# A block's transposes moved into the next block's x projection, and a group's scores moved behind the gate

## The chip, the cores and the metric

The kernel runs on one core of one Trainium2 chip. The metric is the device time of one execution in microseconds, as the median of several runs. All times below are of one core.

## The reference, cut to what matters

The program is one layer of a hybrid model on 4 sequences of 256 tokens with 512 channels (1024 tokens in all): causal attention with 32 heads and an adapter, a small gated feed-forward layer, a state-space mixer with 128 heads of 64 channels in 8 groups, and the feed-forward layer again. The change lies in the mixer. There the reference computes:

```python
proj = input_states @ in_proj_w.T            # gate | x, B, C | dt
xBC  = silu(conv(xBC) + conv_b)              # causal, 4 taps, each channel for itself
...
scores  = einsum('bcihn,bcjhn->bcijh', C, B) * Ldec * dt
y_intra = einsum('bcijh,bcjhp->bcihp', scores, xc)
...                                          # plus the state carried between chunks, plus D * x
g = y * silu(gate)
g = g * rsqrt(mean(g * g over the group) + eps) * norm_w
return g @ out_w.T
```

B and C belong to a group of 16 heads; Ldec is the exponential of differences of cumulated decays. The kernel computes the state-space part over a whole sequence as one masked product: scores of C and B, times exponentials of decay differences, times x scaled by dt.

## The kernel before, in words

**Blocks and groups.** The mixer's 8192 channels are 64 blocks of 128 channels, two heads each (`NB`); 8 blocks make a group (`GB`). For block `i`, `g` is its group and `gi` its place in the group, 0 to 7. The activations lie channel by token, 128 x 1024 to a tile. float32 products are made of three matmuls on split operands (`mm3`, lines 115 to 117), so that a projection of 128 channels is 2 halves (512 tokens each) of 12 matmuls of 128x512.

**What a block does**, in the order in which `block(i)` writes it:

- the x projection (`projected("x", i, ...)`), two halves into a PSUM tile `pp` of two; between the halves it calls what it was given;
- `conv`: ScalarE's first tap (L964), VectorE's three taps (L971), ScalarE's Silu (L975) give `x2`;
- in blocks with `gi` 2 to 6, and in all of group 0, the output products `outer` of the group before (24 matmuls into `pog`, slots of tag "m", added to x by L1115), and around them `inner_products(i - 1)`: 32 matmuls of 128x64 weights (L1044, tile `pyy`) and then `gated` (L1054 to L1067);
- the gate projection (`projected("g", i, between)`). In the blocks with `gi` 7, 0 and 1 of later groups (`late`) `between` runs `inner_products(i - 1)` and `outer` between the gate's halves;
- the Silu of the gate (L1211), and `differences` of the two heads: VectorE (L1004), a mask on GpSimd (L1008) and exponentials on ScalarE (L1013, L1014, L1016) in `em`;
- `turned(i, x2)`: 8 transposes of x2 on TensorE (L1027, tile `trx`, two slots of tag "m"), and two VectorE multiplies by dt into `xd` (L1030);
- in blocks with `gi` 3 and 4 the B or C projection and convolution of the next group (`convolved`);
- `weighted`: `em` times the group's scores `gm` (L1020).

**Scores.** A group's `scores` are four pairs of matmuls (L986, L990, tile `pg`, slots of tag "m"), each followed by a VectorE multiply into `gm` (L991). They belong to the first block of a group (`gi` 0): two pairs between the x halves, two between the gate halves, ahead of the products of the block before.

**Order.** In group 0 a scheduler orders all engines. From block 8 on TensorE's instructions stand in the order written (`manual_schedule`), while the scheduler orders VectorE, ScalarE, GpSimd and SP's loads by its own forecast of the times. Every engine works through its own order and waits where an input or a slot is missing. The "m" slots are two, for `trx`, `pg`, `pog` and the sums `pqs`; `xd` has one buffer, `em` four, `x2` two.

**Tables.** ScalarE's Silu, exponential and square root need different function tables; a change between them is an ACT_TABLE_LOAD.

Of the kernel before, what the change touches and what calls it, by code (L numbers as in the profile page):

```python
# [29 lines left out]
NB = INTER // P  # L30
# [49 lines left out]
def hybrid_kernel(  # L80
# [12 lines left out]
    x = keep.tile([P, TT, C], F32, name="x")  # L93
# [11 lines left out]
    def split(hl, v, engine=nc.vector):  # L105

        nc.scalar.copy(hl[0], v)  # L107
        engine.tensor_tensor(hl[1], v, hl[0].bitcast(F32), ALU.subtract)
# [20 lines left out]
    class Norm:  # L129
# [33 lines left out]
        def turn(self, xn, tr, xs):  # L163

            for k in range(KC):
                nc.tensor.transpose(tr[:, k, :], xn[:, k * P : (k + 1) * P], ident)
            split(xs, tr)
# [618 lines left out]
    def mixer(feed, later):  # L786
        with ExitStack() as es, ExitStack() as inner:
# [25 lines left out]
            def prepare(i):  # L813

                for n in range(i, i + 3):
                    fetch(n)
                if i < NW and i not in pieces:
                    pieces[i] = [pw.tile([P, KC, P], F32R, name=f"w{j}", tag=f"w{j}") for j in range(2)]
                    split(pieces[i], raws.pop(i), nc.gpsimd if i < 18 or order[i][1] % GB in (7, 0) else nc.vector)

            def project(w, pp, cols):
                mm3(pp[:, cols], [[v[:, k, :] for v in w] for k in range(KC)],
                    [[v[:, k, cols] for v in xs] for k in range(KC)])
# [137 lines left out]
            def conv(pp, ch, tag, bufs):  # L961

                acc = (po_ if tag == "gb" else p2).tile([P, NT], F32, name="acc", tag=tag, bufs=bufs)
                nc.scalar.activation(  # L964
                    acc, pp, AF.Identity, bias=cb_s[:, ch : ch + 1], scale=cw_s[:, ch, 3:4]
                )
                av = acc.rearrange("p (b t) -> p b t", b=B)
                pv = pp.rearrange("p (b t) -> p b t", b=B)
                for tap in range(3):
                    d = 3 - tap  # L970
                    nc.vector.scalar_tensor_tensor(  # L971
                        av[:, :, d:], pv[:, :, : L - d], cw_s[:, ch, tap : tap + 1], av[:, :, d:],
                        ALU.mult, ALU.add,
                    )
                silus.append(nc.scalar.activation(acc, acc, AF.Silu).ins)  # L975
                return acc
# [45 lines left out]
            def turned(n, x2):  # L1022

                xd = p2.tile([P, TT, P], F32, name="xd", tag="xd", bufs=1)
                trs = [ps.tile([P, 4, P], F32, name="trx", tag="m") for _ in range(2)]
                for c in range(TT):
                    nc.tensor.transpose(trs[c // 4][:, c % 4, :], x2[:, c * P : (c + 1) * P], ident)  # L1027
                for half, tr in enumerate(trs):
                    hs = slice(half * 4, half * 4 + 4)
                    nc.vector.tensor_tensor(  # L1030
                        xd[:, hs, :].rearrange("p c (h d) -> p c h d", h=2),
                        tr.rearrange("p c (h d) -> p c h d", h=2),
                        dt_t[:, hs, 2 * n : 2 * n + 2].unsqueeze(3).to_broadcast([P, 4, 2, PD]),
                        ALU.mult,
                    )
                return xd

            def product(xd, es2):
                py = ps_y.tile([P, B, L], F32, name="pyy", tag="pyy")
                for b in range(B):  # L1040
                    for k in range(2):
                        for hh in range(2):
                            d = slice(hh * PD, (hh + 1) * PD)
                            nc.tensor.matmul(  # L1044
                                py[d, b, k * P :], xd[:, 2 * b + k, d],
                                es2[hh][:, b, 2 * k : 2 if k == 0 else 3, :].rearrange("p s i -> p (s i)"),
                                start=(k == 0), stop=(k == 1),
                            )
                return py
# [77 lines left out]
            def projected(kind, n, between=lambda: None):  # L1127
                i = at[kind, n]
                prepare(i + 1)
                prepare(i + 2)  # L1130
                w = pieces.pop(i)
                if i == 0:
                    return first[1]
                pp = (
                    ps_y.tile([P, NT], F32, name="pp", tag="pyy") if (kind, n) == ("g", 0)
                    else ps_p.tile([P, NT], F32, name="pp", tag="pp")
                )
                for half in range(2):
                    project(w, pp, slice(half * 512, half * 512 + 512))
                    if half == 0:  # L1140
                        between()
                return pp
# [7 lines left out]
            def outer():  # L1150

                q, t, hl = recalled.pop(0)
                po = ps.tile([P, C], F32, name="pog", tag="m")
                for half in range(2):
                    partial(po, q, hl[half], half)
                if t == 0:
                    rgs[q] = root(sqs.pop(q))
                scaled(q, t, po)

            def inner_products(m):  # L1160
                px2, gt, xd, em = stage.pop(m)
                py = product(xd, em)
                sqs[m // GB] = gated(m, px2, gt, py, sqs.get(m // GB))
# [8 lines left out]
            stage, sqs, wos, rgs, todo = {}, {}, {}, {}, []  # L1172
            recalled = []
            PER = {1: 1, 2: 2, 3: 1, 4: 1, 5: 2, 6: 1}
            def block(i, scoring, gm):
                g, gi = divmod(i, GB)
                if gi == 0 and g:
                    scoring = scores(group["b"], group["c"])
                    gm = next(scoring)
                    todo.extend((g - 1, t) for t in range(TT))  # L1180

                def scored():

                    for _ in range(2 if gi == 0 and g else 0):
                        next(scoring)

                x2 = conv(projected("x", i, scored), i, "x2", 2)

                late = gi in (7, 0, 1) and g > 0
                if not late:
                    if recalled:
                        outer()
                    if i:
                        inner_products(i - 1)
                    while recalled:
                        outer()
                if gi == 6:
                    wos.setdefault(g, []).extend(out_weights(g, k) for k in range(3))  # L1200

                def between():
                    scored()
                    if late:
                        inner_products(i - 1)
                        while recalled:
                            outer()

                pp = projected("g", i, between)
                gt = p2.tile([P, NT], F32, name="gt", tag="gt", bufs=1)  # L1210
                nc.scalar.activation(gt, pp, AF.Silu)  # L1211
                em = []
                for h in (2 * i, 2 * i + 1):
                    with tc.issue_after(silus[2]) if i == 0 else ExitStack():
                        em.append(differences(h, rr.pop(h)))
                    if h + 2 < H:
                        rr[h + 2] = rows(h + 2)
                xd = turned(i, x2)
                if gi in NEXT and g + 1 < G:
                    convolved(NEXT[gi], g + 1)  # L1220
                for e in em:
                    weighted(e, gm)
                stage[i] = (x2, gt, xd, em)
                for _ in range(PER.get(gi + 1, 0)):
                    if todo:
                        q, t = todo.pop(0)
                        recalled.append((q, t, [recall(q, t, half) for half in range(2)]))
                if gi == 7:
                    wos[g].extend(out_weights(g, k) for k in range(3, 6))
                if gi == 0 and g:  # L1230
                    wos[g - 1].extend(out_weights(g - 1, k) for k in range(6, 8))
                return scoring, gm
# [3 lines left out]
            with tc.manual_schedule(engines={nc.tensor.engine}):  # L1236
                for i in range(GB, NB):
                    scoring, gm = block(i, scoring, gm)
            inner_products(NB - 1)
            wos[G - 1].extend(out_weights(G - 1, k) for k in range(6, 8))  # L1240
            es_p.close()
# [48 lines left out]

    later = ExitStack()
    mixer(attention(later), later)


# [67 lines left out]
```

## Time and profile before

| | |
|---|---|
| runs | 1895.62, 1890.53, 1892.50 us; median 1892.5 |
| profiled execution | 1893.48 us; span from the first to the last instruction 1891.7 us, mean granted TensorE clock 0.987 |
| attention and feed-forward, up to the mixer's first block | about 410 us |
| mixer, blocks 0 to 7 | about 410 to 540 us |
| mixer, blocks 8 to 63 | about 540 to 1805 us, 181 us for a group of 8 blocks in groups 2 to 5 |
| rest (last output products, feed-forward) | about 1805 to 1892 us |

The page gives the busy time of each engine over the whole span. As TensorE's order is fixed from block 8 on, a gap on TensorE has one cause: the next instruction in its order lacks an input or a slot. In a timeline the time of a step is best read from the start of one matmul to the start of the next, since the ends of matmuls are modelled.

### The profile page before, as it was taken

To read this page: it belongs to the slowest core of one execution; us is meant where nothing else is said; L and a number is where in the kernel's file an instruction comes from. 1 tells how busy PE (TensorE), PEld (TensorE's weight loads), DVE (VectorE), ACT (ScalarE), POOL (GpSimd) and SP (SyncE) were. 2 spreads that over 40 slices of the span, in tenths; PEclk is the share of its full clock that TensorE was granted. 3 is DMA by queue.
4 is the path that set the end of the run, shared out by engine and by line. 5 is a ranking of instruction groups with operands and counts; after the bars stand their busy time and mean duration, and the time that the engine had idled before them with its cause. 6 is when DMAs were issued, how large, how long until landed. Compare 5 with 4: busy or idle time off the path is not lost.

```text
span 1891.7 us, 29927 instructions
## 1 busy us (share of the span) xinstructions
PE 1806.6 (96%) x10706; PEld 1454.4 (77%) x10706; DVE 1503.3 (79%) x2272; ACT 1425.3 (75%) x2851; POOL 459.7 (24%) x425
## 2 busy tenths in 40 slices
PE   8999988899999999999999999999999999999997
PEld 6777767677778887787788778877887788788777
DVE  5576667689998878887998788869878987897767
ACT  6666675379999768877887787778777976897654
POOL 6332230014442122212211311121222211321200
PEclk9999989899999999999999999999999999999999
DMA  4000000034565445543554455445544543554341
GB/s 143 1 1 1 22 15 25 24 101 156 172 199 184 142 135 170 175 150 124 177 184 144 141 161 176 148 143 167 170 134 155 184 152 123 165 186 156 101 120 54
DMA packets 152773, 240.35 MB, mean 127 GB/s; under 512 B 12464, under 2 KB 77616, under 8 KB 152624
## 3 DMA queue, kind: packets, MB, share of 16 engines
q1 hardware_dynamic: 152624, 238.44, 39.3%
q8 instruction: 84, 1.38, 0.3%
q14 instruction: 65, 0.53, 0.1%
HBM read 202.75 MB, written 35.65 MB: 126 GB/s over the span
## 4 chain that ended last, share of the span: by engine, by line
PE 61%; ACT 14%; DVE 13%; DMA 4%; issue 4%; POOL 3%; SPq 0%; DVEq 0%; ACTq 0%; POOLq 0%
PE pp L115 8%; PE pp L116 8%; PE pp L117 8%; PE pyy L1044 6%; PE pog L115 6%; PE pog L116 6%; PE pog L117 6%; DVE acc L971 3%; DMA wor<-in_wout_dram 2%; ACT e L477 2%; PE trx L1027 2%; DVE em L1020 1%; POOL sq L1067 1%; ACT em L1016 1%; ACT em L1013 1%
## 5 line engine op out<-in xcount | busy, mean ns | idle before, releaser
L115 PE MATMUL pp<-mx,w 128*128 128x512 f32 (+1 forms) x1160 | 463.7, 400 | 4.8 <-DVE acc L971 3.0
L116 PE MATMUL pp<-mx,w 128*128 128x512 f32 (+1 forms) x1160 | 452.4, 390 | 0.0
L117 PE MATMUL pp<-mx,w 128*128 128x512 f32 (+1 forms) x1160 | 452.3, 390 | 0.0
L971 DVE SCALAR_TENSOR_TENSOR acc<-pp,cw_s,acc 128x1012 f32<-128x1012 f32 (+2 forms) x240 | 303.8, 1270 | 70.1 <-ACT acc L964 67.9
L1020 DVE TENSOR_TENSOR em<-em,gm 128x1536 f32<-128x1536 f32 x128 | 254.6, 1992 | 40.1 <-ACT em L1016 40.1
L1008 POOL TENSOR_SCALAR_AFFINE_SELECT r<-r 128x512 f32<-128x512 f32 x128 | 127.2, 995 | 629.3 <-DMA r<-cumd 488.8
L115 PEld LDWEIGHTS pp<-mx,w 128*128 128x128 f32 x1160 | 219.1, 189 | 54.7 <-issue 8.3
L117 PEld LDWEIGHTS pp<-mx,w 128*128 128x128 f32 x1160 | 218.7, 189 | 46.4 <-issue 0.6
L116 PEld LDWEIGHTS pp<-mx,w 128*128 128x128 f32 x1160 | 219.2, 189 | 41.3 <-issue 0.6
L1067 POOL TENSOR_TENSOR sq<-sq,acc 128x1024 f32<-128x1024 f32 x55 | 149.7, 2722 | 355.1 <-ACT acc L1066 355.1
L115 PE MATMUL pog<-wo,gh 128*128 128x512 f32 x512 | 202.6, 396 | 0.0
L116 PE MATMUL pog<-wo,gh 128*128 128x512 f32 x512 | 199.5, 390 | 0.0
L117 PE MATMUL pog<-wo,gh 128*128 128x512 f32 x512 | 199.5, 390 | 0.0
L1004 DVE TENSOR_SCALAR em<-r,col_t 128x128 f32<-128x128 f32 x512 | 168.1, 383 | 28.3 <-PE pyy L1044 22.2
L1044 PE MATMUL pyy<-em,xd 128*64 128x256 f32 (+1 forms) x2048 | 183.4, 330 | 0.8 <-DVE em L1020 0.8
L1044 PEld LDWEIGHTS pyy<-em,xd 128*64 128x64 f32 x2048 | 129.9, 137 | 59.6 <-issue 17.5
L1013 ACT ACTIVATE em<-r,col_t 128x128 f32<-128x128 f32 x512 | 169.6, 391 | 6.2 <-PE pyy L1044 5.2
L1016 ACT ACTIVATE em<-r,col_t 128x128 f32<-128x128 f32 x512 | 170.3, 390 | 1.6 <-POOL r L1008 1.3
L107 ACT CAST w<-wr 128x512 fp32r<-128x512 f32 x144 | 88.4, 614 | 83.2 <-PE pp L116 79.6
L477 ACT ACTIVATE e<-sc,nmx 128x256 f32<-128x256 f32 (+1 forms) x256 | 104.2, 442 | 21.0 <-DVE nmx L471 20.9
L107 ACT CAST gh<-gr 128x512 fp32r<-128x512 f32 (+1 forms) x128 | 76.5, 607 | 52.8 <-PE pog L116 42.4
L115 PEld LDWEIGHTS pog<-wo,gh 128*128 128x128 f32 x512 | 96.1, 188 | 22.9 <-issue 3.8
(290 smaller groups left out, 3291.1 us busy)
## 6 DMA issues: line engine op xcount, KB each, us to landing
wr<-in_win_dram SPq DMA_DIRECT2D x287, 256.0 KB, 2.7
r<-cumd SPq DMA_DIRECT2D x128, 512.0 KB, 4.1
spill<-gb SPq DMA_DIRECT2D x63, 512.0 KB, 2.9
gr<-spill SPq DMA_DIRECT2D x120, 256.0 KB, 3.1
wor<-in_wout_dram SPq DMA_DIRECT2D x64, 256.0 KB, 3.6
out_dram<-x SPq DMA_DIRECT2D x8, 256.0 KB, 2.3
x<-in_x_dram SPq DMA_DIRECT2D x1, 1536.0 KB, 9.0
gr<-spill SPq DMA_DIRECT2D x8, 192.0 KB, 2.8
```

The lines of the kernel that those rows point to most:

```text
L107: nc.scalar.copy(hl[0], v)
L115: nc.tensor.matmul(o, lh, rh, start=(first and k == 0), stop=False)
L116: nc.tensor.matmul(o, lh, rl, start=False, stop=False)
L117: nc.tensor.matmul(o, ll, rh, start=False, stop=(last and k == n - 1))
L477: nc.scalar.activation(es_[c][:, 2 * j + pr, :], sc[:, j, :], AF.Exp, bias=nm[:, j : j + 1], accum_out=rs[:, c, h : h + 1],)
L971: nc.vector.scalar_tensor_tensor(av[:, :, d:], pv[:, :, : L - d], cw_s[:, ch, tap : tap + 1], av[:, :, d:], ALU.mult, ALU.add,)
L1004: nc.vector.tensor_scalar(e[:, b, 2, :], rv[:, b, 1, :], col_t[:, h, b, 1:2], 0.0, ALU.subtract, ALU.min,)
L1013: nc.scalar.activation(e[:, b, 1, :], rv[:, b, 1, :], AF.Exp, bias=col_t[:, h, b, 2:3])
L1016: nc.scalar.activation(e[:, b, 0, :], rv[:, b, 0, :], AF.Exp, bias=col_t[:, h, b, 0:1])
L1020: nc.vector.tensor_tensor(e, e, gm, ALU.mult)
L1044: nc.tensor.matmul(py[d, b, k * P :], xd[:, 2 * b + k, d], es2[hh][:, b, 2 * k : 2 if k == 0 else 3, :].rearrange("p s i -> p (s i)"), sta ...
L1067: (nc.gpsimd if n < NB - 1 else nc.vector).tensor_tensor(sq, sq, x2, ALU.add)
```

## The change

The transposes and the xd multiplies of a block, from group 1 on, are no longer issued after that block's gate projection but between the two halves of the next block's x projection. The block's entry in `stage` has three parts until then, and four afterwards. The last block has no next one: its `turned` comes after the loop. In group 0 nothing is moved.

A new group's scores are no longer issued between the x halves (two pairs) and between the gate halves (two pairs), but between the gate halves (two pairs) and behind the gate (two pairs). No instruction of TensorE, VectorE or GpSimd is added or removed.

```diff
-                x2 = conv(projected("x", i, scored), i, "x2", 2)
+                def turn():
+
+                    if i - 1 in stage and len(stage[i - 1]) == 3:
+                        px2, pgt, pem = stage[i - 1]
+                        stage[i - 1] = px2, pgt, turned(i - 1, px2), pem
+
+                x2 = conv(projected("x", i, turn), i, "x2", 2)
...
                 pp = projected("g", i, between)
+                scored()
                 gt = p2.tile([P, NT], F32, name="gt", tag="gt", bufs=1)
                 nc.scalar.activation(gt, pp, AF.Silu)
...
-                xd = turned(i, x2)
+                xd = [turned(i, x2)] if g == 0 else []
                 if gi in NEXT and g + 1 < G:
                     convolved(NEXT[gi], g + 1)
                 for e in em:
                     weighted(e, gm)
-                stage[i] = (x2, gt, xd, em)
+                stage[i] = (x2, gt, *xd, em)
...
             with tc.manual_schedule(engines={nc.tensor.engine}):
                 for i in range(GB, NB):
                     scoring, gm = block(i, scoring, gm)
+            px2, pgt, pem = stage[NB - 1]
+            stage[NB - 1] = px2, pgt, turned(NB - 1, px2), pem
             inner_products(NB - 1)
```

## The prediction

> **What bounds the kernel now.** I read the engine shares of the page first, then the waits of TensorE, then the timeline of one such wait, then busy time by stretch.
>
> ```profile
> PE 1806.6 (96%) x10706; PEld 1454.4 (77%) x10706; DVE 1503.3 (79%) x2272; ACT 1425.3 (75%) x2851; POOL 459.7 (24%) x425
> ```
>
> TensorE carries the span. Inside the mixer its 128x512 matmuls start 0.227 us apart, and in most blocks nothing interrupts them, so only two things can shorten this part: fewer matmuls, or the few places where TensorE stands. The view of TensorE's waits (sum in us, times, longest):
>
> ```profile
> PE trx L1027 <- ACT acc L975: 20.7, 11, 3.0
> ...
> PE trx L1027 <- DVE x L1115: 2.6, 6, 0.4
> ```
>
> Two rows of L1027, the transposes of x2, hold nearly all of the mixer's idle time. The timeline of TensorE around one wait (start, duration, then in brackets the idle time and what ended it), block 31:
>
> ```profile
> 1081.23 0.39 PE L117 MATMUL pp<-mx,w 128*128 128x512 f32 x1
> 1083.60 1.09 PE L1027 MATMUL trx<-con,acc 128*128 128x128 f32 x8 [1.98 <-ACT acc L975]
> 1084.45 0.47 PE L115 MATMUL pp<-mx,w 128*128 128x512 f32 x1
> ```
>
> From the last gate matmul to the first matmul of the next projection 3.22 us pass. In an undisturbed block it is 1.03 us (start 1066.47 to 1067.50 in block 30), so this block loses 2.19. The transposes are late because the Silu of x2 (L975) is; ScalarE's timeline of the same place:
>
> ```profile
> 1074.46 1.19 ACT L964 ACTIVATE acc<-pp,cb_s,cw_s 128x1024 f32<-128x1024 f32 x1
> ...
> 1078.70 1.28 ACT L1013 ACTIVATE em<-r,col_t 128x128 f32<-128x128 f32 x4 [0.85 <-PE pyy L1044]
> 1079.89 0.97 ACT L1016 ACTIVATE em<-r,col_t 128x128 f32<-128x128 f32 x3
> 1081.19 1.28 ACT L975 ACT_TABLE_LOAD   x1 [0.33 <-DVE acc L971]
> 1082.49 1.06 ACT L975 ACTIVATE acc<-acc 128x1024 f32<-128x1024 f32 x1
> ```
>
> The x projection ended at about 1073.0 and the Silu at 1083.55: the chain is 10.6 us. TensorE has only 8.5 us of other work for it in this block (gate half 2.72, products of block 30 3.1, gate half 2.72).
>
> Measured so for every block 8 to 62, the loss over 1.03 us is: gi = 7 (blocks 15, 23, ... 55) 3.99, 2.12, 2.19, 2.27, 2.19, 3.38, together 16.1; gi = 0 (16 to 56) 0.05, 0.32, 1.47, 1.32, 1.42, 0, together 4.6; gi = 1 (9 to 57) 0.74, 0.90, 0.91, 0.89, 0.87, 0.87, 0, together 5.2, where the transposes wait for a slot that L1115 frees; gi = 2 to 6: 0. Sum **25.9 us**. Block 63 loses another 4.0.
>
> **What the Trainium skill says.** "TensorE: Matmul & The Clock Gate", section "Step-by-step: what each phase is for": matmuls stay in program order, only weight loads are pulled ahead. The trace agrees: at 1081.6 the next x projection, whose inputs are ready, stands 2 us behind the transposes. Same page, "What's actually happening": after an idle window of about 3.4 us the clock is halved. The trace agrees: after the waits of 3.17 us (block 15) and 2.84 us (block 55) matmuls start 0.43 us apart for a while, and the granted clock of the stretch 718 to 727 is 0.81. "ScalarE: Activation LUTs", "What ACT_TABLE_LOAD costs": 1283 ns for the load and 1380 ns of drain. The trace has 1283 ns a load, and the next function starts 1.30 us after the load's start (1081.19, 1082.49), so 1.28 is used here. "Perfetto Trace Analysis", "Optimization Strategy": a gap that repeats can mean too few buffers; here that holds only for the 2.6 us of L1115.
>
> **The change part by part.** Nothing is computed more or less: 8 transposes and two xd multiplies a block, four score pairs a group and every DMA stay. The built order of instructions shows what moves.
>
> (a) **Transposes of block i go between the x halves of block i+1** (blocks 8 to 62). Ahead of them now stands another half projection, 12 x 0.227 = 2.72 us. A wait of up to 2.72 us is gone: the waits themselves were 2.06 to 2.21 us in blocks 23 to 47, 3.17 in 15 and 2.84 in 55, so 0.45 + 0.12 = 0.6 us is left. With the wait under the idle window the slow clock goes as well; its cost inside the 1.03 us is already in the 25.9, and the slow matmuls after it add 0.75 (block 15) and 1.15 (block 55). The waits of gi = 0 and gi = 1 (at most 1.4) are wholly covered. At gi = 0 the chain has even more room, since two score pairs (0.65 us each) also come first. Block 63 has no successor: its 4.0 us stay. Switching from 512-wide matmuls to transposes and back costs the same wherever it happens. **-25.9 - 1.9 + 0.6 = -27.2.**
>
> (b) **Scores** move from between the x halves to between the gate halves, and from there to behind the gate. In block 8 the first pair waited 0.9 us for slots; there the wait goes: **-0.9**. What comes later is gm (L991, 0.54) and the two weightings of gi = 0 (L1020, 1.99). From the last score to the products that need them lie half, transposes, half, half = 2.72 + 1.03 + 2.72 + 2.72 = 9.2 us. VectorE's order there is two L991, a split, two L1020, two xd: the weightings end about 0.5 + 0.6 + 3.4 = 4.5 us after the last score, xd at about 5.8. Margin 3.4 us: cost 0.
>
> (c) **xd comes later, so its slots do.** A pair of PSUM slots (tag "m") is shared by transposes, scores and the output partial sums pog.
>
> ```profile
> L1030 DVE TENSOR_TENSOR xd<-trx,dt_t x128: 672/678/693, 419.7 to 1801.6; 128x512 f32<-128x512 f32 x128
> ```
>
> Before, the next user of a slot came a whole projection (5.45 us) after the transposes. Now in gi = 2 to 6 (35 blocks) pog comes one half, 2.72 us, after them, and the product needs both xd 8.2 us after. Two xd take 1.36 us, so VectorE must start the first within 2.0 us. The tightest place is gi = 4 and 5, where xd stands behind two taps of the group's B or C convolution: from that projection's end L964 1.20, tap 1.27, split 0.68, tap 1.27, xd 0.68 = 5.1 us, against the deadline 2.72 + 1.03 + 2.72 = 6.5. Margin 1.4 us. In gi = 2, 3 and 6 a weighting or a split stands ahead whose inputs are ready about when the transposes are. Bounds: 0 if always in time, 12 blocks x 1.3 us = 16 us if one table load always falls into gi = 4 and 5. I take 2.
>
> (d) **ScalarE's order changes.** Counting table loads in the built programs, the mixer has 223 before and 258 after: in groups 1 to 6 one more at gi = 3, two at gi = 4, two at gi = 5, one at gi = 6 (one fewer once). 35 x 1.28 = 45 us more work on ScalarE. The stretches of busy time (PE, PEld, DVE, ACT, POOL, then clock, DMA share, GB/s) of gi = 7 to 1, gi = 2 to 6, and of gi = 4 and gi = 5 alone:
>
> ```profile
> 1066.50:1126.40 59.90, 56.20 (x331) 44.84 (x329) 51.74 (x66) 51.62 (x85) 16.36 (x10) 1.00 0.53 171
> 1126.40:1249.00 122.60, 122.60 (x657) 99.20 (x656) 99.36 (x129) 93.61 (x168) 22.39 (x18) 1.00 0.48 151
> 1172.20:1197.80 25.60, 25.60 (x138) 20.74 (x137) 21.25 (x27) 20.30 (x34) 3.62 (x4) 1.00 0.46 144
> 1197.80:1228.90 31.10, 31.10 (x163) 25.30 (x162) 26.27 (x32) 23.83 (x45) 5.28 (x6) 1.00 0.48 150
> ```
>
> gi = 4 and 5 go from 20.3 to 22.9 of 25.6 and from 23.8 to 26.4 of 31.1 us on ScalarE: it keeps 11 and 15% idle. No price on the path; bounds 0 and 45 us.
>
> (e) **SP and POOL.** The loads of r and wr change places by one or two near each block's end, and the mask L1008 by one; numbers and sizes stay. POOL is busy 24% and DMA a half of the time: cost 0, bounds -1 and +2.
>
> Sum against the profiled execution, 1893.5 us (span 1891.7 and 1.8 around it): -27.2 - 0.9 + 2 = -26.1, so 1867.4. That execution stands 1.0 over the median of 1892.5, so **1867 us** for the median.
>
> **Rivals.** *Part is given back* (c): xd or a tap is late at gi = 4 and 5 by a table load, up to 16 us, 1870 to 1883; for it speaks the margin of 1.4 us, against it the idle 11%.
>
> *The engines behind TensorE are the bound at the group's border, so the wait only moves* to the products or to pog: of the border's 59.9 us VectorE and ScalarE are busy 51.7 and 51.6; without the 4.55 us of waits it is 55.4, 93% for both. Against it: gi = 2 runs VectorE 23.9 of 25.6 us (93%) and TensorE doesn't wait once. It would give 1892. The same time comes if the build had left the transposes where they were, but its order shows them moved.
>
> *Slower: ScalarE's table loads reach TensorE.* Place: gi = 3 to 6, where exps and Silus now alternate. Each load pushes L964 or the exps of em, VectorE's in-order queue stands at that instruction, xd behind it is late, and pog waits for its slot. All 35 would cost 45 us, 1893.5 - 28.1 + 44.9 = 1910; it decides from 63% of them (28 us) on. Against it: a load of 1.28 us is shorter than the margins, except where two fall ahead of one tap.
>
> **How the numbers follow.** Waits covered: 1862 to 1874, chance 0.66. Part given back: 1874 to 1887, 0.14. The wait moves: 1887 to 1898, 0.07. Table loads reach the path: 1898 to 1915, 0.13. A measurement of this kernel tells about 0.3% (5.7 us) from no change, so faster is 0.66 + 0.14 = 0.80, same 0.07, slower 0.13. The range of 8 in 10 is 1861 to 1889: the low end has no new wait and a little over the 28.1 us back, the high end takes in (c) whole and the beginning of the moved wait.
>
> **What would show it.** Right: no wait of trx for L975 or L1115 in blocks 8 to 62, 1.03 us around every transpose group, clock 1.00 around 720 and 1625, one wait of about 3 us left in block 63, ACT_TABLE_LOAD up by 35. (c) wrong: waits of pog for xd (L1030), or of pyy for xd or em, at gi = 2 to 6. Wrong altogether: the same 25 us under other names at gi = 7 to 1, or matmuls further apart than 0.227 us at gi = 4 and 5 in every group.

## Result and profile after

The changed kernel takes 1883.08 us as the median of 7 runs (1879.47 to 1887.77), the kernel before 1893.40 us in the 7 runs beside it. The ratio is 0.9949, 95% interval 0.9932 to 0.9965: 10 us faster, where 26 were forecast. The profiled execution took 1881.98 us (span 1880.2, mean granted clock 0.989); that of before had a span of 1891.7, so the two traces that are compared here lie 11.5 us apart.

The busy time of the engines on the page after:

```profile
PE 1802.6 (96%) x10706; PEld 1449.8 (77%) x10706; DVE 1516.1 (81%) x2272; ACT 1467.9 (78%) x2886; POOL 452.0 (24%) x425
```

TensorE has as many matmuls as before. ScalarE has 35 instructions more, all of them table loads, and 42.6 us more work. The view of TensorE's waits, cut to the stretch from 540 to 1780 us (blocks 8 to 62; sum in us, times, longest):

```profile
PE pp L115 <- ACT gt L1218: 8.3, 5, 1.7
PE trx L1027 <- ACT acc L975: 4.7, 5, 1.7
PE pog L115 <- DVE xd L1030: 0.8, 1, 0.8
```

In the same stretch of the kernel before, the row of trx for L975 has 17.8 us in 10 waits (20.7 in 11 over the whole span); here it is 4.7 in 5. That of L1115 is gone. But a row is on top that was not there before: a gate projection that waits for the Silu of a gate (L1218, L1211 before) to free its `pp` tile. By the distances from start to start, all transpose groups of gi = 7 take 1.03 us now: the 16.1 us there and the slow clock after blocks 15 and 55 are gone (the granted clock of the stretch 718 to 727 is 1.00, before 0.81). The new losses lie at gi = 0 and 1 in five of the six groups that have such a border after 700 us: the transposes of block gi = 0, which now stand in the x projection of gi = 1, lose 1.82, 0.72, 0.65, 1.93 and 0.59 us (blocks 16, 24, 32, 40, 56), together 5.7; the gate projection of gi = 1 behind them loses about 1.8 each time, together 9.1.

One such place, block 33, in the timeline of TensorE after:

```profile
1098.18 0.39 PE L117 MATMUL pp<-mx,w 128*128 128x512 f32 x1
1099.01 1.09 PE L1027 MATMUL trx<-con,acc 128*128 128x128 f32 x8 [0.44 <-ACT acc L975]
1099.85 0.49 PE L115 MATMUL pp<-mx,w 128*128 128x512 f32 x1
...
1102.49 0.39 PE L117 MATMUL pp<-mx,w 128*128 128x512 f32 x1
1104.52 0.50 PE L115 MATMUL pp<-mx,w 128*128 128x512 f32 x1 [1.64 <-ACT gt L1218]
```

From 1098.18 to 1099.85 are 1.67 us where 1.03 would do; from 1102.49 to 1104.52 are 2.03 where 0.227 would do. Both waits name ScalarE. ScalarE's timeline of the same place shows that it was not busy but stood still:

```profile
1086.48 1.19 ACT L964 ACTIVATE acc<-pp,cb_s,cw_s 128x1024 f32<-128x1024 f32 x1
...
1088.08 0.40 ACT L1016 ACTIVATE em<-r,col_t 128x128 f32<-128x128 f32 x1
...
1095.60 0.99 ACT L1013 ACTIVATE em<-r,col_t 128x128 f32<-128x128 f32 x3 [4.25 <-DMA r<-cumd]
1096.60 1.28 ACT L975 ACT_TABLE_LOAD   x1
1097.89 1.06 ACT L975 ACTIVATE acc<-acc 128x1024 f32<-128x1024 f32 x1
...
1103.44 1.02 ACT L1218 ACTIVATE gt<-pp 128x1024 f32<-128x1024 f32 x1
```

Three exponentials (L1013) of block 33's first head stand ahead of the Silu of block 32. They need `r`, the row of cumulated decays of that head, and wait 4.25 us for its load. The Silu's own last input, VectorE's third tap, is ready long before, at 1092.83:

```profile
1091.56 1.27 DVE L971 SCALAR_TENSOR_TENSOR acc<-pp,cw_s,acc 128x1020 f32<-128x1020 f32 x1
```

Its table load starts at 1096.60, 3.8 us after that, and the gate's Silu stands behind it. The same three exponentials wait for `r` at all six borders after 700 us: 4.2 to 5.6 us at the five where TensorE loses time, and 1.85 us at block 48, where it loses none. SP's timeline shows why the load is late:

```profile
1087.57 2.74 SPq L811 DMA_DIRECT2D wr<-in_win_dram  x2
1090.40 0.38 SPq L996 DMA_DIRECT2D r<-cumd  x1
```

A buffer of `r` is freed by the last L1016 that reads it, at 1088.08 + 0.40. In the new order L964 stands ahead of this L1016; and on SP two loads of wr stand ahead of the load of `r`, so that it is issued at 1090.40, 1.9 us after the buffer is free. It lands 5.1 us later. Before, the same load and the same exponential were:

```profile
1092.54 0.33 SPq L996 DMA_DIRECT2D r<-cumd  x1
```

```profile
1094.11 1.19 ACT L964 ACTIVATE acc<-pp,cb_s,cw_s 128x1024 f32<-128x1024 f32 x1
...
1101.41 1.06 ACT L975 ACTIVATE acc<-acc 128x1024 f32<-128x1024 f32 x1
...
1103.78 0.40 ACT L1013 ACTIVATE em<-r,col_t 128x128 f32<-128x128 f32 x1
```

The load of `r` went out 1.6 us ahead of L964 and landed in 3.8 us, and the exponentials that need it stood behind the Silu.

The account, from the start of one block's products (pyy) to the next, after against before: 2.5 of the 11.5 us lie ahead of the products of block 6, where the change does nothing. From there to the products of block 63 the changed kernel gains 8.9 us. The intervals that hold the transposes of gi = 7 are 24.5 us shorter, 7.3 of it because two score pairs (1.22 us in each of six groups) now fall into the next interval, so **-17.2**. The next intervals (x and gate projection of gi = 1) are 19.4 us longer, without those 7.3 **+12.1**: here the new waits of 5.7 and 9.1 us outweigh the 4.6 us that were lost before, which makes 10.2 of the 12.1; the rest was not followed. After that come -4.6 (the slot wait that L1115 ended), +2.4 behind the transposes of gi = 2, -0.6 at the border from group 0 to 1 and -1.1 at block 63. All other intervals are equal to 0.0 us.

### The profile page after: what moved, and what is told of

It is laid out like the page before. It is cut to its first block, busy times and chain, and to the rows that moved or that the text cites. A ratio compares the mean times of both kernels' runs of the same rounds, so it can differ in the third digit from the quotient of the medians.

```text
span 1880.2 us, 29875 instructions
## 1 busy us (share of the span) xinstructions
PE 1802.6 (96%) x10706; PEld 1449.8 (77%) x10706; DVE 1516.1 (81%) x2272; ACT 1467.9 (78%) x2886; POOL 452.0 (24%) x425
## 4 chain that ended last, share of the span: by engine, by line
PE 59%; DVE 15%; ACT 14%; DMA 5%; issue 5%; POOL 1%; SPq 0%; ACTq 0%; DVEq 0%; POOLq 0%
PE pp L115 8%; PE pp L116 7%; PE pp L117 7%; PE pog L115 6%; PE pyy L1044 6%; PE pog L116 6%; PE pog L117 6%; DVE acc L971 4%; DVE em L1004 3%; DMA r<-cumd 3%; ACT e L477 2%; PE trx L1027 1%; ACT L1218 1%; ACT em L1016 1%; ACT em L1013 1%
## 5 line engine op out<-in xcount | busy, mean ns | idle before, releaser
L971 DVE SCALAR_TENSOR_TENSOR acc<-pp,cw_s,acc 128x1012 f32<-128x1012 f32 (+2 forms) x240 | 304.8, 1270 | 56.5 <-ACT acc L964 54.5
L1020 DVE TENSOR_TENSOR em<-em,gm 128x1536 f32<-128x1536 f32 x128 | 248.1, 1948 | 39.6 <-ACT em L1016 39.5
L1008 POOL TENSOR_SCALAR_AFFINE_SELECT r<-r 128x512 f32<-128x512 f32 x128 | 121.5, 950 | 655.1 <-DMA r<-cumd 496.4
L1067 POOL TENSOR_TENSOR sq<-sq,acc 128x1024 f32<-128x1024 f32 x55 | 144.7, 2632 | 334.7 <-ACT acc L1066 334.7
L1013 ACT ACTIVATE em<-r,col_t 128x128 f32<-128x128 f32 x512 | 170.0, 391 | 43.5 <-DMA r<-cumd 25.6
L1004 DVE TENSOR_SCALAR em<-r,col_t 128x128 f32<-128x128 f32 x512 | 180.3, 405 | 28.6 <-PE pyy L1044 15.0
L1016 ACT ACTIVATE em<-r,col_t 128x128 f32<-128x128 f32 x512 | 167.9, 390 | 0.4
L108 DVE TENSOR_TENSOR gh<-gr,gh 128x512 fp32r<-128x512 f32 (+1 forms) x128 | 110.8, 874 | 7.8 <-ACT gh L107 7.3
```

The lines of the kernel that those rows point to most:

```text
L971: nc.vector.scalar_tensor_tensor(av[:, :, d:], pv[:, :, : L - d], cw_s[:, ch, tap : tap + 1], av[:, :, d:], ALU.mult, ALU.add,)
L1004: nc.vector.tensor_scalar(e[:, b, 2, :], rv[:, b, 1, :], col_t[:, h, b, 1:2], 0.0, ALU.subtract, ALU.min,)
L1008: nc.gpsimd.affine_select(rv[:, :, 0, :], rv[:, :, 0, :], pattern=[[0, B], [1, P]], compare_op=ALU.is_ge, fill=-1e30, base=0, channel_mult ...
L1013: nc.scalar.activation(e[:, b, 1, :], rv[:, b, 1, :], AF.Exp, bias=col_t[:, h, b, 2:3])
L1016: nc.scalar.activation(e[:, b, 0, :], rv[:, b, 0, :], AF.Exp, bias=col_t[:, h, b, 0:1])
L1020: nc.vector.tensor_tensor(e, e, gm, ALU.mult)
```

## Experiments: where the rest of the gain went

The theory: at a group's border the exponentials ahead of the Silu wait for the load of `r`, and that alone makes the new waits. It was tested from two sides, and then with both.

**The exponentials of gi = 1 held behind the Silu of gi = 0.** A scheduling constraint that puts ScalarE's instructions of `differences`, the exponentials, behind the given one; `silus[-1]` is the Silu of the block's x2.

```diff
+                held[0] = held[1]
                 x2 = conv(projected("x", i, turn), i, "x2", 2)
+                held[1] = silus[-1]
...
-                    with tc.issue_after(silus[2]) if i == 0 else ExitStack():
+                    with tc.issue_after(silus[2]) if i == 0 else tc.issue_after(held[0]) if gi == 1 and g else ExitStack():
```

> The changed kernel with one constraint on ScalarE: in blocks gi = 1 of groups 1 to 7 the exponentials of that block are issued after the Silu of x2 of the block before. The built order then has no exponential waiting for r ahead of that Silu, 252 table loads. Theory A: no wait of the transposes at gi = 0, no wait of the gate projection at gi = 1 for the gate's Silu, about 15 us less than the changed kernel: 1866 to 1871 us, 0.986 to 0.988 of the kernel before. Theory B: the work on ScalarE is the same but for 6 table loads, so 1876 to 1884. Theory C: nothing changes, 1883.

Measured: 1871.39 us (1867.96 to 1875.32), ratio to before 0.9889 (0.9872 to 0.9906), against 0.9949 for the changed kernel: 11.7 us faster than that, 0.4 over theory A's range and far from the others. ScalarE's timeline at the same border:

```profile
1089.59 1.28 ACT L975 ACT_TABLE_LOAD   x1 [1.55 <-DVE acc L971]
1090.89 1.06 ACT L975 ACTIVATE acc<-acc 128x1024 f32<-128x1024 f32 x1
...
1093.77 0.41 ACT L1013 ACTIVATE em<-r,col_t 128x128 f32<-128x128 f32 x1
```

The Silu waits for its own last input again, VectorE's third tap, and L1013 comes behind it without a wait for `r`. TensorE's waits for the gate's Silu fall from 8.9 us to 0.5.

**ScalarE's order at the border left alone, and `r` loaded earlier.** `r` becomes two tiles of half the size, one for each chunk, with two buffers each. The half that L1013 reads is free before the L1016s are done.

```diff
-                r = p2.tile([P, NT], F32, name="r", tag="r", bufs=2)
-                load(r, cumd[h : h + 1, :].to_broadcast([P, NT]))
-                return r
+                v = cumd[h : h + 1, :].rearrange("h (b c i) -> h b c i", b=B, c=2)
+                out = []
+                for c in (1, 0):
+                    r = p2.tile([P, B, P], F32, name=f"r{c}", tag=f"r{c}", bufs=2)
+                    load(r, v[:, :, c, :].to_broadcast([P, B, P]))
+                    out.append(r)
+                return out
```

> The changed kernel with r loaded in two tiles of 256 KB, one for the second 128 tokens of each sequence (read by L1004 and L1013, free early), one for the first (read by the mask and L1016). ScalarE's built order at the border is that of the changed kernel, three exponentials ahead of the Silu of x2; but the half of r that they need has a free slot about a block earlier, and its load stands ahead of two wr loads. 128 more loads on SP. Theory A: the 4 us wait of L1013 for r is gone in every group, and with it 14 to 15 us: 1867 to 1872 us. Theory B: 1880 to 1886. Theory C: 1883.

Measured: 1874.21 us (1871.83 to 1877.86), ratio 0.9909 (0.9894 to 0.9925), 8.9 us faster than the changed kernel and 2 over what was expected. SP, and ScalarE at the same border (L1017 is L1013 here):

```profile
1082.90 0.43 SPq L999 DMA_DIRECT2D r<-cumd  x1
1086.80 3.03 SPq L811 DMA_DIRECT2D wr<-in_win_dram  x2
```

```profile
1091.91 0.98 ACT L1017 ACTIVATE em<-r,col_t 128x128 f32<-128x128 f32 x3
1093.16 1.28 ACT L975 ACT_TABLE_LOAD   x1 [0.27 <-DVE acc L971]
```

The load now goes out ahead of the two wr loads. The same three exponentials stand ahead of the Silu as in the changed kernel and wait for nothing. So it was the load and not their 0.98 us of work. From the products of gi = 7 to the next ones, the stretch that became longer in the changed kernel, this version is 16.0 us shorter than the changed kernel, the one with the constraint 12.3. What keeps it behind that one all the same are waits of pog for xd (6.3 us in 5).

**Both together.**

> The changed kernel with both mends of before: r in two tiles, and at gi = 1 the exponentials behind the Silu of x2. Theory A (the late load of r ahead of the Silu is one cause, mended by either): no further gain over either alone, 1868 to 1875 us. Rival (two separate causes, each mend took away one): the gains of 12 and 9 us add up, 1860 to 1864.

Measured: 1867.94 us (1867.30 to 1868.66), ratio 0.9867 (0.9845 to 0.9889). The two gains of 11.7 and 8.9 give 15.1 and not 20.6: they mostly remove the same wait. The time is a hair under theory A's range, and the rival's sum, 1860 to 1864, did not come. This is the fastest version. In the stretch behind the products of gi = 7 it gains 16.0 us, no more than with `r` in halves alone; most of its lead over that version, 7.7 us, lies where pog waited for xd and no longer does. From 540 to 1800 us TensorE's waits are 4.3 us for L971 (of which 3.2 are at block 8), 2.1 at the transposes of block 63, and 0.3.

**Fewer table loads.** The constraint of the first experiment in all blocks of groups 1 to 7 (`if g` in place of `if gi == 1 and g`).

> As the run in which the exponentials of gi = 1 stand behind the Silu of x2, but in all blocks of groups 1 to 7: each block's exponentials are issued behind the Silu of x2 of the block before. 216 table loads in the mixer instead of 252, so 46 us less work on ScalarE. If table loads in gi = 3 to 6 cost nothing on the path (step d of the prediction): 1868 to 1874 us, as with gi = 1 alone. If they do cost: 1855 to 1866. A later em can also make the products late in some blocks: then above 1875, with waits of pyy for em.

Measured: 1872.77 us (1871.74 to 1874.40), ratio 0.9894 (0.9874 to 0.9914). ScalarE has 36 instructions and 46.7 us less than in the version with gi = 1 alone (busy 1414.6 against 1461.3), and the time is the same within the intervals. But the constraint moves the exponentials too: waits of pog for xd grow from 0.7 to 3.1 us, and 0.53 us in each of five groups are new behind the products of gi = 3, while the border gains. So the run shows that the sum of the loads doesn't set the time, not what each load costs.

**The same with `r` in halves.**

> The version with the Silu held ahead at gi = 1 and the load of r in halves, with the Silu held ahead in all blocks of groups 1 to 7 (37 fewer table loads, 47 us of ScalarE's work). If ScalarE's total work is off the path, as in the kernel with that order and whole loads of r: 1866 to 1873, no better than 1867.9. If part of the wait of pog for xd that is left comes from table loads: 1860 to 1865.

Measured: 1878.08 us (1875.53 to 1884.20), ratio 0.9926 (0.9902 to 0.9951): 10 us slower than with the constraint at gi = 1 alone, outside both expectations. ScalarE's timeline at the Silu of block 31 (gi = 7):

```profile
1077.68 0.72 ACT L1083 ACTIVATE wo<-wor,nw_s 128x512 fp32r<-128x512 f32 x1 [4.96 <-DMA wor<-in_wout_dram]
...
1079.72 1.06 ACT L975 ACTIVATE acc<-acc 128x1024 f32<-128x1024 f32 x1
```

With the exponentials out of the way the scheduler put a scaling of the output weights (L1083, L1079 before) ahead of the Silu. It waits 4.96 us for its load, and the transposes of gi = 7, not those of gi = 0, wait for their Silu (12.6 us in 8, with blocks 6 and 63). It is the same fault with another load, one block earlier.

## Experiments: the two halves of the change

**Transposes alone, scores where they were.**

```diff
-                x2 = conv(projected("x", i, turn), i, "x2", 2)
+                def both():
+                    scored()
+                    turn()
+
+                x2 = conv(projected("x", i, both), i, "x2", 2)
...
-                scored()
                 gt = p2.tile([P, NT], F32, name="gt", tag="gt", bufs=1)
```

> The changed kernel with its scores put back (two pairs between the x halves, two between the gate halves); only the transposes are moved. In its built order ScalarE has no exponential of the next block ahead of the Silu of x2 at gi = 0, but 279 table loads in the mixer (before 223, changed kernel 258). Theory A (a late load of r holds exponentials that stand ahead of that Silu, and so holds the transposes of gi = 0 and the gate of gi = 1): those waits are absent, 1865 to 1872 us, about 0.987 of the kernel before. Theory B (ScalarE is simply full at the group's border, table loads count): 21 more loads than the changed kernel, so 1883 or more. Theory C (the scores behind the gate make gm and xd late): 1865 to 1872 too.

Measured: 1921.64 us (1920.70 to 1929.11), ratio 1.0173 (1.0152 to 1.0193): 29 us slower than before. Of the expectations only theory B's open one, 1883 or more, holds this number; its reason is taken up below. TensorE's waits:

```profile
PE trx L1027 <- DVE gm L991: 16.9, 8, 3.0
PE pog L117 <- DVE gh L108: 7.2, 7, 1.2
...
PE pog L115 <- ACT gh L107: 4.5, 6, 1.1
```

In the first block of a group the transposes now stand right behind two score pairs, which hold both "m" slots until L991 has read them. Four of the eight waits are about 3 us. In the matmuls after the one of 2.99 us (block 40):

```profile
1285.27 1.72 PE L1027 MATMUL trx<-con,acc 128*128 128x128 f32 x8 [2.99 <-DVE gm L991]
...
1287.21 0.63 PE L116 MATMUL pp<-mx,w 128*128 128x512 f32 x1
1287.64 0.63 PE L117 MATMUL pp<-mx,w 128*128 128x512 f32 x1
```

the starts are 0.43 us apart instead of 0.227, and the granted clock is 0.50 from 1285.6 to 1288.9. So such a wait costs some 1.5 us more than its length, by an estimate from these starts and the slow transposes. This followed three of the four waits of 3 us. Why L991 is late at all, in VectorE's timeline of the same place:

```profile
1282.10 2.56 DVE L1004 TENSOR_SCALAR em<-r,col_t 128x128 f32<-128x128 f32 x2
1284.58 0.54 DVE L991 TENSOR_TENSOR gm<-pg,tri 128x384 f32<-128x384 f32 x1
```

The first scores are complete by about 1281.6, but two L1004 stand ahead of L991, and one of the two takes 2.37 us; the usual is 0.27. GpSimd at that time:

```profile
1281.98 2.40 POOL L1067 TENSOR_TENSOR sq<-sq,acc 128x1024 f32<-128x1024 f32 x1 [1.13 <-ACT acc L1066]
```

L1004 ends when this addition ends. The Trainium skill, "SBUF — State Buffer", section "SBUF: two separate sides", says that VectorE and GpSimd share one pair of SBUF ports, which is locked for a whole instruction while the other engine stands; on VectorE's side this holds for its two-port modes and for two SBUF inputs. The trace fits this, with 2.37 against 0.27 us: all 27 L1004 of more than 1 us in blocks 8 to 63 end about 0.1 us after an instruction of GpSimd. That L1004 runs in such a mode is not shown.

**Scores alone, transposes where they were.** In the kernel before, `scored` is called between the gate's halves and behind the gate.

> The kernel before with the scores moved as in the change; the transposes stay where they were. Theory A: the waits of gi = 7 (about 2.2 us a group) and gi = 1 (0.9) stay, those of gi = 0 shrink by the 1.3 us of two pairs ahead of the transposes (about 4 us in all): 1888 to 1892 us. Theory B: the same. Theory C: the scores' own cost shows, 1893 to 1905 us.

Measured: 1908.10 us (1906.46 to 1914.13), ratio 1.0089 (1.0074 to 1.0105), 16 us slower and over all three expectations. TensorE's waits:

```profile
PE trx L1027 <- ACT acc L975: 17.2, 8, 3.0
PE trx L1027 <- DVE gm L991: 11.2, 9, 2.4
```

The waits of gi = 7 are untouched. Added are waits of the transposes of gi = 0 for a slot, since they now follow the second two score pairs directly, and at gi = 1 for the slot of the group's sums (L1093, 4.2 us in 6). So each half alone puts transposes and scores next to each other; only the two together keep a half projection between them.

**Transposes ahead of the scores.** The first half again, with `turn()` called before `scored()`.

> The kernel with only the transposes moved (1921.6 us), but between the x halves of gi = 0 the transposes go ahead of the two score pairs instead of behind them; the built order of ScalarE has 279 table loads in both. Theory D (there the transposes and the scores want the same two slots one right behind the other, and transposes stand until VectorE has made gm): the wait of transposes for L991 is gone; instead the first pair waits for xd, about 1 us a group, and the waits in gi = 2 stay: 1900 to 1912 us. Rival (ScalarE's 279 table loads make it slow): 1915 to 1925, the same as before the swap.

Measured: 1921.89 us (1913.26 to 1930.49), ratio 1.0149 (1.0121 to 1.0177), as slow as the other order, as the rival had it. Theory D's wait of 1 us a group came out at 2 under the name that it expected: pg for xd (L1030) 14.1 us in 7, where trx for gm had 16.9. The waits of pog behind the transposes of gi = 2 stayed. Two pairs of users meet in two slots, in either order.

**Transposes moved in all blocks but gi = 7**, so that none stands beside scores (`turned` stays behind the gate for gi = 7), and **transposes moved everywhere, with the exponentials held behind the Silu** in groups 1 to 7:

> The transposes moved alone (scores as in the kernel before), in all blocks but the last of a group (gi = 7), whose transposes stay behind that block's own gate, so that they don't meet the score pairs in the first block of the next group. Table loads stay many (50 more than before). Theory S (the slots at the border): the waits of trx for gm are gone, the 16 us of gi = 7 of before are back, the waits of gi = 0 and 1 are gone: 1880 to 1895. Theory T (table loads): the waits of pog at gi = 2 and the slow stretches after them stay, and the time is 1905 to 1925.

> The transposes moved alone (scores as in the kernel before), but in groups 1 to 7 the exponentials of a block are held on ScalarE until behind the Silu of the block before it. The transposes alone took 1921.6 us, with 56 more table loads than before; this order has 42 fewer than that one, 14 more than before. Theory T (the table loads, 1.28 us each, put ScalarE's work late, and that is why the transposes alone were slow): at least half of the 29 us over before comes back, 1885 to 1905, and the waits of pog for the split of gr (L107, L108) and for xd at gi = 2 go. Theory S (score pairs and transposes meet in the two slots of tag m at a group's border, and the order of the exponentials has nothing to do with it): the 3 us waits of trx for gm (L991) in blocks 16, 24, 32, ... stay, with the slow clock after them, and the time stays at 1912 to 1925.

Measured: 1907.50 (1899.94 to 1908.77), ratio 1.0073 (1.0048 to 1.0098), and 1908.52 (1900.25 to 1913.31), ratio 1.0080 (1.0049 to 1.0112). Neither theory had it alone. The first number lies in theory T's range, but its waits at the border are those of theory S: without the meeting the waits of trx for gm fall from 16.9 to 1.1 us, and waits of trx for L975 are back with 16.9. The second number lies between the two. With the other order of exponentials the waits of pog for gh fall from 11.7 to 0.5 us, and 13.5 us of trx for gm stay.

**GpSimd's addition left out for gi = 6**, so that the group's sum of squares lacks one block of eight, with the orders of the other engines as they were, once with the transposes alone and once with the exponentials held:

```diff
-                    (nc.gpsimd if n < NB - 1 else nc.vector).tensor_tensor(sq, sq, x2, ALU.add)
+                    if n % GB != GB - 2:
+                        (nc.gpsimd if n < NB - 1 else nc.vector).tensor_tensor(sq, sq, x2, ALU.add)
```

> The transposes moved alone (scores as in the kernel before), and GpSimd's addition into the group's sum of squares (L1067) left out for the block with gi = 6 of each group: one addition of 2.4 us a group, so that the sum lacks one block of eight. The orders of VectorE, ScalarE and TensorE are the same as with the transposes alone (1921.6 us). Theory P: at the group's border one VectorE decay difference (L1004) takes 2.37 us instead of 0.27 because it runs beside this addition, L991 stands behind it, and the slots that the transposes need come 2 us late; each wait of 3 us also slows the matmuls after it (some 1.5 us). Then L1004 takes 0.27 us there, the waits of trx for gm fall from 16.9 to about 5 us, and the time falls by 12 to 20 us, to 1901 to 1910. Rival: the long L1004 has another cause (a late semaphore, a late r) and stays; 1916 to 1926.

> The same addition left out (the sum of squares lacks the block with gi = 6 of each group) in the version with the transposes moved alone and the exponentials held behind the Silu in groups 1 to 7 (1908.5 us), with the orders of VectorE, ScalarE and TensorE unchanged. Theory P: the waits of trx for gm fall from 13.5 to 3 to 6 us and the time to 1892 to 1901, so that the border's slots and the table loads are two separate parts of what the transposes alone cost. Rival: the waits stay, 1904 to 1912.

Measured: 1906.55 us (1899.46 to 1907.20), ratio 1.0054 (1.0034 to 1.0073), and 1891.10 us (1884.37 to 1898.87), ratio 0.9992 (0.9979 to 1.0005). One addition of 2.4 us a group, on an engine that is busy 23% of the time, is worth 15 and 17 us by the medians (22 and 17 by the ratios). In the first of the two, the same two L1004 as above, and the transposes behind them:

```profile
1277.64 0.47 DVE L1004 TENSOR_SCALAR em<-r,col_t 128x128 f32<-128x128 f32 x2
```

```profile
1278.73 1.23 PE L1027 MATMUL trx<-con,acc 128*128 128x128 f32 x8 [0.88 <-DVE gm L991]
```

The wait went from 2.99 to 0.88 us and the slow matmuls behind it are gone; over the run, trx for gm falls from 16.9 to 6.9 us, and with the exponentials held from 13.5 to 2.8. That x2 comes free earlier without the addition is not the cause: ScalarE's L964 waits for GpSimd's additions 1.4 us in all in the one run and 1.2 us in the other. So the 29 us that the transposes alone cost are about half GpSimd's addition beside L1004 and half the order of the exponentials, and the two add up. Whether the second half is the table loads themselves (42 fewer) or which exponentials come first was not told apart.

## Why the prediction was right or wrong

**Sign and mechanism of (a): right at gi = 7 and for the slot.** Forecast were -16.1, -1.9 of slow clock and +0.6 that stays, together -17.4; measured are -17.2. The parts are not quite those: the 0.6 us didn't stay, and two short waits of a projection for VectorE's taps (L971), 0.57 and 0.43 us by the starts, came. The wait for L1115 was to give 5.2 and gave 4.6. Block 63 kept its wait. The reason given for the clock was not tested here, since the waits before it went to nothing; the runs of the halves speak against it (last section).

**Size: the steps that failed are (e), and in (a) the sentence that the waits of gi = 0 and gi = 1 "are wholly covered", where it speaks of the Silu of gi = 0.** For that Silu -4.6 us were forecast and +12.1 came: a difference of 16.7 us, nearly the whole distance between the 26.1 that were forecast and the 8.9 that these blocks gave. Step (e) saw that loads of r and wr change places and priced it at 0, bounds -1 and +2, because POOL and the DMA queues have idle time. Idle time of a queue says nothing on the place of one load in it: this load was issued behind two others, and the exponentials ahead of the Silu stood until it landed. Without that (exponentials held, `r` in halves) 15.1 us come back. Step (a) took the chain of the Silu of gi = 0 as it was before and gave it more room. The order of ScalarE had changed under it, and I counted in (d) how many table loads that makes and did not ask what the instruction just ahead of the Silu waits for.

**(b): right in the changed kernel.** The 0.9 us are gone, and outside block 63 no product waits for the weightings by more than 0.5 us a time. But the cost of 0 holds only because the transposes move as well: alone, this part costs 16 us.

**(c): right in size, not in place.** Its price was 2 us, feared at gi = 4 and 5. Measured are 2.4 us behind the transposes of gi = 2 (one wait of pog for xd of 0.8 us, and about 0.27 us in each of five groups, where pog starts 0.15 us after the first xd), and none at gi = 4 and 5.

**(d): right in what decides it here.** 35 loads were counted and 35 came. 36 loads taken out again, 46.7 us of ScalarE, left the time the same, with some other waits in place of the old ones.

**The rivals.** *Part is given back* names the time that came, 1883, but not the cause: it wanted late xd at gi = 4 and 5, and nothing waits there. *The wait only moves* comes nearest: 14.8 us of waits came back at the border, under the names of the gate's Silu and of L975. Its reason, that VectorE and ScalarE are full there, doesn't hold, since ScalarE stood idle for 4.25 us just then. *Table loads reach TensorE* did not happen. The fastest version's 1867.94 us is nearly the forecast number, which doesn't make the forecast right: that kernel holds an order and splits a load, and the change does neither. (The forecast's own sum, 1867.4 less 1.0, gives 1866.4, not 1867.)

## What to carry to other kernels

When a change lets a scheduler order the other engines anew, look, for each instruction that the bound engine waits for, at what now stands directly ahead of it in its queue and what that one's last input is; where it is a load, look at what stands ahead of the load on its issuing queue. A count of the added work doesn't show this: here 46.7 us of ScalarE's work could go without a gain, and one late load at five of six borders cost about 15 us. Two moves can each be slower alone and faster together when they share two slots, so a test of one half says little on the whole.

## What was not expected of the hardware

- A VectorE tensor-scalar of 128x128 took 2.37 us beside GpSimd's addition of 128x1024, and 0.27 us otherwise. Taking out that addition alone gave 15.1 us (1921.64 to 1906.55). It need not cost time: in the fastest version 33 L1004 of blocks 8 to 63 take more than 1 us, and the two waits of TensorE in blocks 9 to 62 (0.75 and 0.31 us, for VectorE's taps) have none of them just ahead.
- A wait of 2.99 us on TensorE was followed by matmuls 0.43 us apart (transposes alone, granted clock 0.50 from 1285.6 to 1288.9). One of 3.02 us in the same run was not (1.00 from 911.6 to 915.5), while one of 1.96 us with the scores alone was (0.50 from 1091.7 to 1095.0). So the clock is halved here after waits that are clearly shorter than the window of about 3.4 us that the prediction reads as confirmed, and the length of a wait alone does not decide it. What else does was not looked for.
- The load of `r` (512 KB as it lands in SBUF) took 5.1 us from issue to landing where it was late (issued at 1090.40), and 3.8 us at the same place before; the median of the changed kernel is 3.9.
